# Attention layer of a four-layer image kernel: packed query and key projections, Ln and Exp for the root, a new order of the steps

## The chip, the core and the metric

The kernel runs on one core of a Trainium2 chip. A core has a matrix engine (PE, with the loading of its weights shown apart as PEld), a vector engine (DVE), a scalar engine (ACT), GpSimd (POOL) and a sync engine (SP) that here only starts transfers. Each engine takes its instructions in order. They share an on-chip memory of 128 partitions (SBUF); PE writes its results to a second memory, PSUM, which has eight banks of 512 floats per partition. The metric is the device time of one execution in microseconds.

## The reference

Four layers work on eight images of 56 x 56 positions with 192 channels. Each is a residual step over a group norm: `x = x + layer(group_norm(x))`. The change lies in layer 1, a shifted-window attention with 64 windows of 7 x 7 = 49 positions per image and 6 heads of 32 channels:

```python
x = (x - mu) * jax.lax.rsqrt(var + EPS) * gamma + beta     # over the channels of a position
sx = jnp.roll(x, shift=(-3, -3), axis=(1, 2))              # then cut into windows of 49
qkv = (win @ w_qkv + b_qkv).reshape(-1, N, 3, HEADS, hd).transpose(2, 0, 3, 1, 4)
attn = jnp.einsum('bhnd,bhmd->bhnm', q * scale, k) + bias + mask
attn = jax.nn.softmax(attn, axis=-1)
out = jnp.einsum('bhnm,bhmd->bhnd', attn, v)               # heads side by side again
out = out @ w_proj + b_proj                                # windows put back, rolled back
```

Layer 0 is a gated Toeplitz convolution, layer 2 a depthwise convolution with running averages, layer 3 a convolution with a two-step perceptron.

## The kernel before

The layers run one after the other, with their intermediate images in device memory. Layer 0 has two stages. In the first (`layer0_qv`) products of two projections are made and stored to the arrays `left` and `right`; in the second (`layer0_mix`) blocks of them are loaded (`lt`, `rt`, L454), rearranged by POOL, ACT and DVE (L462), multiplied on PE (L470), and gated and projected (L480 to L579). At the start of `layer0_mix` two blocks are loaded, two operands of each kind are prepared, the large tiles `os` are laid out, and then the weights `w_p` and `w_o` are fetched by POOL's queue (L110). A tile laid out where a tile of the stage before lay must wait for the last user of that place.

**Layer 1** holds an image as 128 rows: two halves of the picture (called streams, s = 0 and 1) of 64 channel rows each, with three channel blocks j in the free dimension. An image is worked off in four groups g; a group has 8 windows in each stream. `layer1_norm` prepares an image ahead of time: `windows` copies and scales it into window order (POOL, and others for the first image), `squares` squares it (ACT), two sets of matmuls with ones (L838, L842, "stat") give sums, `finish` turns the variance into 1/root (L813 on DVE, L815 Sqrt on ACT, L817 reciprocal on DVE), and `scaled` spreads the factors by a matmul (L822) and multiplies (L827, DVE). It is a generator: each `next` does one small piece.

Attention of a group is cut into steps, named by letters:

- Q: one projection of queries or keys for 3 of the 6 heads, 96 output rows, both streams (L880); four of them per group. Query results get their bias and are both copied by ACT (L886); key results go by ACT and DVE (L888, L890).
- V: one of two projections of values (L898), copied by ACT and DVE (L905, L907).
- E: scores of one stream, 48 small products (L916) into the PSUM tile S; then on DVE the added bias and mask (L922) and the maximum (L924), and on POOL the subtraction (L925). E0 is the first, E1 the second.
- X: exponents of one stream (L929, ACT). Y: their sum and its reciprocal (L934, L935, DVE) and the multiplication by it (L936, POOL).
- T: one third of a stream's turn, four transposes (L957) and a copy by ACT or DVE (L962, L964). The first turn of stream 0 is called T0 below.
- P: the mix of values by shares (L971), into two PSUM tiles, one for each half z of the windows, copied by ACT and DVE (L982, L984).
- R: the output projection of one channel block j (L990), then added into the image on DVE (L998) in two pieces, since the roll wraps around. R0, R1, R2 are the three.
- G: statistics of a block of the finished group before (L1001, DVE). There are three of them for a group; a G that finds none left does nothing.
- N: one piece of the next image's norm.

Within a group, Q, V and E already belong to the next group, while X, Y, T, P and R belong to the present one. The order on every engine of this stage is the order in which the program writes the instructions, and that is a string:

```python
plan = "X Q Y V X G Q Y N T T T N Q N P N G V N N T T T N G N N P N Q N R N E N R G E N R".split()
```

PSUM is shared out: S has three banks; three buffers called "mm" go round for Q (2), V (2), stat, scaled and R; two called "et" go round for T and P. A matmul that needs a buffer waits until its last contents have been copied out.

`layer1_weights` prepares weights and biases during layer 0. `gn_finish` makes the scale and shift of a group norm.

Of the kernel before, what the change touches and what calls it, by code (L numbers as in the profile page):

```python
# [19 lines left out]
HC = 96  # L20
TT = 392
# [50 lines left out]
    ("g1", 3), ("be1", 3), ("bq", 2), ("bv", 2), ("bpr", 3),  # L72
# [18 lines left out]
def kernel(ctx: ExitStack, tc: tile.TileContext, a: dict, out: bass.AP):  # L91
# [71 lines left out]
    def gn_finish(mv, sc, sh, pool, psum, ptag):  # L163
# [23 lines left out]
        nc.scalar.activation(sc, over_groups(d, "gh_v"), AF.Sqrt, bias=eps5)  # L187
        nc.vector.reciprocal(sc, sc)
# [395 lines left out]
    def layer0_mix(pool, raws, psum, ops, loaded):  # L584
# [63 lines left out]
        n, gate, first, side, xn = 0, iter(()), iter(()), iter(()), None  # L648
        os = [pool.tile([64 + W, 128, H], F32, name=f"o{k}", bufs=1) for k in range(2)]
        w_p, w_o = (resident(n, nc.gpsimd, pool) for n in ("w_p", "w_o"))  # L650
# [48 lines left out]
    def layer1_weights(pool, psum):  # L699
# [9 lines left out]
        bv = pool.tile([HC, 2], F32, name="bv", bufs=1)  # L709
        for which, t in ((0, bq), (2, bv)):  # L710
            ps = psum.tile([128, 2, 512], F32, name="bias", tag="qv")[:, 0]
            for m in range(2):
                c0 = which * C + HC * m
                for j in range(3):
                    nc.tensor.matmul(
                        ps[0:HC, m:m + 1], w_qkv[0:64, j, c0:c0 + HC], vec("be1", j, 64), start=(j == 0), stop=(j == 2)
                    )
            o = VOFF["bq" if which == 0 else "bv"]
            nc.vector.tensor_tensor(t, ps[0:HC, 0:2], vecs[0:HC, o:o + 2], ALU.add)
        nc.vector.tensor_scalar(bq, bq, HD ** -0.5, None, ALU.mult)  # L720
        yield
        ps = psum.tile([128, 2, 512], F32, name="bias", tag="qv")[:, 0]
        for s in range(2):
            for j in range(3):
                for m in range(2):
                    nc.tensor.matmul(
                        ps[64 * s:64 * s + 64, j:j + 1], w_proj[:, m, 64 * j:64 * j + 64], bv[:, m:m + 1],
# [6 lines left out]
        nc.vector.tensor_scalar(w_qkv[:, :, 0:C], w_qkv[:, :, 0:C], HD ** -0.5, None, ALU.mult)  # L734
# [35 lines left out]
    def layer1_norm(b, x, pool, psum, consts, first=False):  # L770
# [41 lines left out]
        def finish(rows):  # L812
            nc.vector.tensor_scalar(rs[rows], rs[rows], 0.0, 1e-5, ALU.max, ALU.add)  # L813
            yield
            nc.scalar.activation(rs[rows], rs[rows], AF.Sqrt)  # L815
            yield
            nc.vector.reciprocal(rs[rows], rs[rows])  # L817
# [11 lines left out]
        for g0, n in ((0, 1), (1, 1), (2, 2)) if first else ((0, 2), (2, 2)):  # L829
            sqs = []  # L830
            for g in range(g0, g0 + n):
                yield from windows(g)
                sqs.append(pool.tile([128, 2, 3, 4 * WN], F32, name="sq", bufs=2))
# [33 lines left out]
    def layer1_scores(g, xr, pool, psum, S, es, consts):  # L867
# [3 lines left out]
        qk = [pool.tile([HC, 2, 2, TT], F32, name=f"qk{s}", bufs=1) for s in range(2)]  # L871
# [3 lines left out]
        def project(which, m):  # L875
            ps = [psum.tile([128, 512], F32, name="qk_ps", tag="mm", bufs=3)[0:HC, 0:TT] for s in range(2)]
# [891 lines left out]
```

## Time and profile before

| | us |
|---|---|
| median of 3 runs | 5577.13 |
| lowest and highest run | 5567.75, 5584.76 |
| profiled execution, its own time | 5579.16 |
| its span, first to last instruction | 5577.4 |

Busy time per engine in four stretches of the span (the second half of layer 1's last group reaches some 10 us into the fourth):

| stretch, us | what | PE | DVE | ACT | POOL | granted clock |
|---|---|---|---|---|---|---|
| 0 to 755 | layer 0, products | 703.3 | 414.4 | 322.4 | 435.9 | 0.98 |
| 755 to 1951 | layer 0, mix | 1087.1 | 563.0 | 601.2 | 631.0 | 0.97 |
| 1951 to 3010 | layer 1 | 957.1 | 628.0 | 392.0 | 396.0 | 0.95 |
| 3010 to 5577 | layers 2 and 3 | 2321.2 | 1428.7 | 974.1 | 415.8 | 0.95 |

In the profile's lines a group is given as line, engine, operation, output <- input, shape, count. In the timeline each row has its start, its busy time, the engine, the line and, in brackets, how long the engine had been idle and what ended the idle time. "xN" counts instructions on the engine: one matmul of the program is two of them. L numbers are lines of the kernel before.

Some durations of layer 1 in this profile: a query copy on ACT 0.58, a key copy 0.48 on ACT and 0.56 on DVE, the root 0.53, the reciprocal of the variance rows 2.55, a table load on ACT 1.28.

### The profile page before, as it was taken

The page shows a single profiled execution, that of the slowest core. Times are in us where ns is not written, and L with a number is a line of the kernel's source. Part 1 is how long each engine was busy: PE and PEld are TensorE (multiplying, and loading weights), DVE is VectorE, ACT ScalarE, POOL GpSimd, SP SyncE. Part 2 cuts the span into 40 slices and gives each one's busy share as a digit, 9 for nine tenths or more (in the row PEclk, how much of TensorE's full clock was granted, in tenths as well). Part 3 has the DMA queues.
Part 4 walks back from the last instruction along what each step waited for, and adds up shares of the span by engine and source line. Part 5 has one row for each costly group of instructions (what it writes and reads, how often), then busy time and mean ns, then how long its engine had stood idle before and what let it go on. Part 6 is the DMA issues. An engine that isn't in the chain of part 4 may idle for free. (4 is left out here: it accounts for less than half of the span.)

```text
span 5577.4 us, 112511 instructions
## 1 busy us (share of the span) xinstructions
PE 5068.6 (91%) x49038; PEld 3354.8 (60%) x49038; DVE 3034.1 (54%) x4087; ACT 2289.7 (41%) x3052; POOL 1878.7 (34%) x1583
## 2 busy tenths in 40 slices
PE   7999969999999889999997989999788787999999
PEld 6788856666666545555554757776344586444444
DVE  4555534555555455655665868888777313333331
ACT  3444445555555333333332015545476402333333
POOL 5555555555555333433432014333111101101000
PEclk9999989999999989999998989999899898999999
DMA  5998996777777512322314856776687596212211
GB/s 150 240 232 225 222 301 247 274 272 274 274 272 274 166 44 72 82 74 72 84 54 101 286 216 218 241 231 200 163 232 217 218 345 263 68 59 82 78 40 27
DMA packets 533281, 1002.69 MB, mean 180 GB/s; under 512 B 256104, under 2 KB 467780, under 8 KB 501412
## 3 DMA queue, kind: packets, MB, share of 16 engines
q1 hardware_dynamic: 519984, 945.57, 52.9%
q0 software_dynamic: 8560, 40.64, 2.2%
q10 hardware_dynamic: 4244, 9.27, 0.6%
q8 instruction: 386, 6.32, 0.5%
q14 instruction: 107, 0.88, 0.0%
HBM read 665.12 MB, written 346.75 MB: 181 GB/s over the span
## 5 line engine op out<-in xcount | busy, mean ns | idle before, releaser
L462 POOL COPY lc<-lt 128x896 f32<-128x896 f32 (+1 forms) x320 | 617.0, 1937 | 491.5 <-PE op L470 485.8
L429 PE MATMUL qv<-w_qv_sb,x 64*112 64x256 f32 (+1 forms) x5376 | 685.5, 408 | 16.1 <-DVE act L435 12.3
L429 PEld LDWEIGHTS qv<-w_qv_sb,x 64*112 64x112 f32 x5376 | 594.7, 175 | 96.0 <-DVE act L435 22.6
L435 DVE TENSOR_TENSOR act<-qv,b_qv 112x640 f32<-112x640 f32 x448 | 318.6, 753 | 319.7 <-PE qv L429 230.3
L439 ACT ACTIVATE act<-act 112x640 f32<-112x640 f32 x448 | 300.4, 683 | 404.9 <-DVE act L435 394.5
L405 POOL TENSOR_TENSOR qv<-act 112x320 f32<-112x320 f32 x448 | 348.8, 805 | 277.3 <-ACT act L439 195.8
L1360 PE MATMUL ph<-y,w_sb 64*128 64x392 f32 x2304 | 397.7, 498 | 6.5 <-ACT hid L1364 6.5
L470 PE MATMUL op<-rc,lc 128*56 128x56 f32 x9216 | 351.9, 220 | 56.3 <-POOL lc L462 37.9
L470 PEld LDWEIGHTS op<-rc,lc 128*56 128x56 f32 x9216 | 327.1, 134 | 125.3 <-POOL lc L462 56.4
L1371 PE MATMUL po<-hid,w_sb 128*64 128x392 f32 x2304 | 386.3, 494 | 0.0
L1378 DVE TENSOR_TENSOR x<-x,z 128x392 f32<-128x392 f32 x96 | 71.6, 746 | 519.7 <-ACT z L1376 519.7
L880 PE MATMUL qk_ps<-xr,wg 64*96 64x392 f32 x1536 | 334.0, 537 | 1.7 <-DVE xr L827 1.7
L1091 PE MATMUL cv<-zc,wt 128*128 128x224 f32 x1536 | 312.9, 355 | 24.1 <-DMA zc<-pd 24.1
L1091 PEld LDWEIGHTS cv<-zc,wt 128*128 128x128 f32 x1536 | 290.4, 189 | 67.5 <-issue 51.4
L925 POOL TENSOR_TENSOR e<-e,mx 128x1176 f32<-128x1176 f32 x64 | 140.0, 2188 | 565.9 <-DVE mx L924 523.1
L1360 PEld LDWEIGHTS ph<-y,w_sb 64*128 64x128 f32 x2304 | 220.0, 188 | 176.0 <-issue 25.6
L503 PE MATMUL y<-pp,w_o_sb 128*64 128x392 f32 x1536 | 309.1, 499 | 6.4 <-DVE pp L497 6.4
L1106 POOL TENSOR_TENSOR rows<-rows,loc 128x896 f32<-128x896 f32 x96 | 220.5, 2297 | 274.0 <-ACT rows L1102 209.2
L480 PE MATMUL pj<-xn,w_p_sb 64*128 64x392 f32 x1536 | 289.3, 509 | 20.8 <-ACT pp L487 18.6
L1371 PEld LDWEIGHTS po<-hid,w_sb 128*64 128x64 f32 x2304 | 162.6, 137 | 213.8 <-issue 213.8
L462 ACT COPY rc<-rt 128x896 f32<-128x896 f32 (+1 forms) x160 | 280.9, 1755 | 19.5 <-DMA rt<-right 19.5
L497 DVE TENSOR_TENSOR pp<-pp,ot 128x784 f32<-128x784 f32 x128 | 124.1, 969 | 293.6 <-PE ot L492 235.0
(242 smaller groups left out, 9034.0 us busy)
## 6 DMA issues: line engine op xcount, KB each, us to landing
lt<-left SPq DMA_DIRECT2D x72, 1792.0 KB
rt<-right SPq DMA_DIRECT2D x72, 1792.0 KB
left<-qv SPq DMA_DIRECT2D x224, 252.0 KB
right<-qv SPq DMA_DIRECT2D x96, 504.0 KB
wt<-in_band_dram SPq DMA_DIRECT2D x23, 2048.0 KB
zc<-pd SPq DMA_DIRECT2D x187, 232.0 KB
pd<-pt SPq DMA_DIRECT2D x7, 5568.0 KB
bm<-bmask SPq DMA_DIRECT2D x64, 588.0 KB
```

Source lines behind the costliest of these rows:

```text
L405: nc.gpsimd.tensor_tensor(qv[:, s, s0:s1, k], *(acts[s][:, which, 0:n].rearrange("p (s d) -> p s d", d=64) for which in range(2)), ALU.mult,)
L429: nc.tensor.matmul(ps[s][:, which, 0:n], x[64 * s:64 * s + 64, j, bass.ts(i, 2 * W)], w_qv[64 * s:64 * s + 64, j, which, 64 * s0:64 * s1], ...
L435: nc.vector.tensor_tensor(acts[s][:, :, 0:n], ps[s][:, :, 0:n], b_qv[:, :, 64 * s0:64 * s1], ALU.add)
L439: nc.scalar.activation(acts[s][:, :, 0:n], acts[s][:, :, 0:n], AF.Silu)
L462: copy(c[:, 0:nu], raw.rearrange("p (w u d) -> p u d w", u=nu, d=64 // nu)[:, :, d0:d0 + 8])
L470: nc.tensor.matmul(op[64 * u:64 * u + W, i, :], lc[:, u, i], rc[:, u, i], start=True, stop=True)
L480: nc.tensor.matmul(ps[:, s, 0:TT], w_p[64 * s:64 * s + 64, j, 128 * c:128 * c + 128], xn[64 * s:64 * s + 64, j, bass.ts(t, TT)], start=(j ...
L503: nc.tensor.matmul(y[64 * s:64 * s + 64], w_o[:, 2 * g + u, 64 * j:64 * j + 64], pp[:, u, s], start=(u == 0), stop=(u == 1),)
L880: nc.tensor.matmul(in_pairs(ps[s]), wg[64 * s:64 * s + 64, j, c0:c0 + HC], in_slots(xr[64 * s:64 * s + 64], (3 * g + j) * GW), start=(j == ...
L1091: nc.tensor.matmul(dst, wt[:, c4 + i, 128 * q:128 * q + 128], zc[:, :, c4 + i, q:q + NPAIR], start=(q == 0), stop=(q == 1),)
L1360: nc.tensor.matmul(ps[:, s, 0:TT], w0[64 * s:64 * s + 64, j, m * 128:(m + 1) * 128], y[64 * s:64 * s + 64, j, ts], start=(j == 0), stop=(j ...
L1371: nc.tensor.matmul(ps[64 * s:64 * s + 64], w1[:, m, 64 * j:64 * j + 64], hid[:, m, s], start=(m == 0), stop=(m == 5),)
```

## The change

Queries and keys are projected in three steps of 128 output rows instead of four of 96. The columns of the weight matrix are reordered by the host so that step 0 gives queries of heads 0 to 2 and the key of head 5, step 1 keys of heads 0 to 2 and the query of head 5, step 2 queries of heads 3 and 4 and keys of heads 3 and 4. ACT copies stream 0's result, DVE stream 1's, both adding the bias. Since a query and its key must stand on the same rows, a further ACT copy within SBUF moves one part of each step into the tiles `q2` and `k2`.

```diff
-        def project(which, m):
+        def project(m):
...
-            for s in range(2):
-                if which == 0:
-                    nc.scalar.activation(qk[s][:, 0, m], ps[s], AF.Identity, bias=bq[:, m:m + 1])
-                elif s == 0:
-                    nc.scalar.copy(qk[s][:, 1, m], ps[s])
-                else:
-                    nc.vector.tensor_copy(qk[s][:, 1, m], ps[s])
+            nc.scalar.activation(qk[:, m, 0], ps[0], AF.Identity, bias=bq[:, m:m + 1])
+            nc.vector.tensor_scalar(qk[:, m, 1], ps[1], bq[:, m:m + 1], None, ALU.add)
+            i, src, dst = ((1, slice(96, 128), slice(64, 96)), (0, slice(96, 128), slice(64, 96)), (1, slice(64, 128), slice(0, 64)))[m]
+            nc.scalar.copy(moved[i][dst], qk[src, m])
...
-            for y, hh, r, p, z in np.ndindex(2, 2, 3, 2, 2):
+            for hh, y, r, p, z in np.ndindex(2, 2, 3, 2, 2):
                 at = WN * (2 * (2 * y + p) + z)
+                rows = slice(HD * r, HD * r + HD)
+                q = moved[0][rows, s] if hh and r == 2 else qk[rows, 2 * hh, s]
+                k = moved[1][rows, s] if hh else qk[rows, 1, s]
```

The mix P puts heads 0 to 3 of one half z on 128 rows and heads 4 and 5 beside them on 64 rows; it goes through the heads by the turn that they come from. Its copies become two per engine. The output projection R takes 128 rows at once and the remaining 64 rows of both halves on different rows of the array, into two PSUM tiles, and its add into the image becomes three pieces.

```diff
-            po = [psum.tile([128, 512], F32, name="po", tag="et", bufs=2)[0:HC, 0:TT] for _ in range(2)]
-            for y, p, hh, r, z in np.ndindex(2, 2, 2, 3, 2):
-                k = 2 * y + p
+            po = [psum.tile([128, 512], F32, name="po", tag="et", bufs=2) for _ in range(2)]
+            for r, y, p, hh, z in np.ndindex(3, 2, 2, 2, 2):
+                k, h = 2 * y + p, 3 * hh + r
+                row, col = (HD * h, 0) if h < 4 else (64 * z + HD * (h - 4), 4 * WN)
...
+                copy(oa[s][:, z], po[z][:, 0:4 * WN])
+                copy(oa[s][rows, 2], po[z][rows, 4 * WN:8 * WN])
...
-            ps = psum.tile([128, 512], F32, name="pr", tag="mm", bufs=3)[:, 0:TT]
-            for m in range(2):
+            out = []
+            for z, (tag, bufs) in enumerate((("mm", 3), ("et", 2))):
+                out.append(psum.tile([128, 512], F32, name=f"pr{z}", tag=tag, bufs=bufs)[:, 0:4 * WN])
                 for s in range(2):
                     nc.tensor.matmul(
...
+                        w_proj[:, 0, 64 * j:64 * j + 64], by_row(oa[s][:, z]), start=True, stop=False,
                     )
...
+            for z in range(2):
+                rows = slice(64 * z, 64 * z + 64)
+                for s in range(2):
+                    nc.tensor.matmul(
+                        out[z][64 * s:64 * s + 64].rearrange("p (i w j) -> p i w j", i=7, j=7),
+                        w_proj[rows, 1, 64 * j:64 * j + 64], by_row(oa[s][rows, 2]), start=False, stop=True,
+                    )
+            for z, w0, w1, c0 in ((0, 0, 28, 3), (1, 0, 25, 31), (1, 25, 28, 0)):
```

The third turn of a stream takes an "mm" buffer instead of an "et" buffer. One over root becomes exp(-0.5 ln v), on ACT alone, in `finish` and, within layer 1, in `gn_finish`; the table that holds both functions is loaded once, at the end of layer 0.

```diff
-            tp = psum.tile([128, 512], F32, name="et_ps", tag="et", bufs=2)
+            tag, bufs = ("mm", 3) if i == 2 else ("et", 2)
+            tp = psum.tile([128, 512], F32, name="et_ps", tag=tag, bufs=bufs)
...
-            nc.scalar.activation(rs[rows], rs[rows], AF.Sqrt)
-            yield
-            nc.vector.reciprocal(rs[rows], rs[rows])
+            nc.scalar.activation(rs[rows], rs[rows], AF.Ln)
+            yield
+            nc.scalar.activation(rs[rows], rs[rows], AF.Exp, scale=-0.5)
...
         layer0_mix(pool, blocks, psum, ops, loaded)
+        nc.scalar.preload_act_table_set("natural_log_exp_and_others")
```

The order string is new, with one Q less and 13 N; in the start of layer 1 one Q goes too. With two groups at once, `layer1_norm` now copies both groups' windows before it squares either. In `layer0_mix` the weights are fetched before the tiles `os` are laid out. `layer1_weights` follows the new order of the columns.

```diff
-        for kind in "QVQVQQEE":
+        for kind in "QVQVQEE":
...
-        plan = "X Q Y V X G Q Y N T T T N Q N P N G V N N T T T N G N N P N Q N R N E N R G E N R".split()
+        plan = "X Q N Y V N X G Q N Y N T T T P N V N N T T T P G Q N R N E N R N G E N R N".split()
...
+        w_p, w_o = (resident(n, nc.gpsimd, pool) for n in ("w_p", "w_o"))
         os = [pool.tile([64 + W, 128, H], F32, name=f"o{k}", bufs=1) for k in range(2)]
-        w_p, w_o = (resident(n, nc.gpsimd, pool) for n in ("w_p", "w_o"))
```

## The prediction

> **What bounds the kernel now.** I read four views, in this order. The page first: the matrix engine is busy 91% of the span, so the question is which of its work shrinks and which waits take its place.
>
> ```profile
> PE 5068.6 (91%) x49038; PEld 3354.8 (60%) x49038; DVE 3034.1 (54%) x4087; ACT 2289.7 (41%) x3052; POOL 1878.7 (34%) x1583
> ```
>
> The chain that ended last carries only 30% of the span and lies in the later layers, so it doesn't price layer 1. Layer 1 runs from 1951 to about 3020 us. I cut one image of it at the end of each E0 (the scores of stream 0), which gives four segments:
>
> ```profile
> 2231.20:2259.25 28.05, 26.59 (x532) 16.27 (x528) 16.94 (x25) 9.77 (x16) 8.76 (x4) 1.00 0.23 67
> 2259.25:2288.57 29.32, 26.91 (x533) 16.45 (x529) 16.93 (x25) 12.07 (x20) 16.92 (x22) 1.00 0.45 111
> 2288.57:2325.90 37.33, 34.20 (x580) 18.91 (x577) 18.65 (x28) 13.85 (x25) 16.21 (x20) 0.91 0.32 78
> 2325.90:2360.58 34.68, 31.56 (x541) 17.81 (x537) 25.39 (x35) 12.27 (x19) 8.75 (x4) 0.95 0.19 54
> ```
>
> The columns are length, then busy time of PE, PEld, DVE, ACT, POOL, then granted clock, DMA share, GB/s. An image is 129.4 us. PE bounds it, but not alone: the plain segment has 1.5 us of PE gaps, and the third and fourth ran partly at half clock (0.91 and 0.95). The timeline of the second segment's first half shows where those gaps come from:
>
> ```profile
> 2262.14 0.74 DVE L998 SCALAR_TENSOR_TENSOR x<-pr,bpr,x 128x371 f32<-128x371 f32 x2
> ...
> 2266.23 1.37 DVE L934 TENSOR_REDUCE sm<-e 128x24 f32<-128x1176 f32 x1
> ...
> 2266.46 2.27 PE L898 MATMUL v_ps<-wg,xr 64*128 64x192 f32 x23 [0.51 <-DVE x L998]
> ...
> 2268.65 2.19 POOL L936 TENSOR_TENSOR e<-e,sm 128x1176 f32<-128x1176 f32 x1
> ...
> 2268.82 2.61 PE L880 MATMUL qk_ps<-xr,wg 64*96 64x392 f32 x11
> ...
> 2271.36 1.09 PE L957 MATMUL et_ps<-ident,e 128*128 128x128 f32 x8
> ```
>
> V waits because its PSUM buffer is the one that R2 used, and DVE empties R2 only after both maxima. T0, the turn of stream 0, needs the chain scores, add, maximum, subtract, exponent, sum, reciprocal, multiply (POOL ends at 2270.84). It starts at 2271.36, 12.1 us after E0's end, because Q1 ended there: PE just outlasts the chain, by about 0.5 us.
>
> **The change on PE.** A project of Q is 2.15 us from start to start (2.22 busy). Four become three: -2.15 per group. R takes 1.59 from start to start. In the new R, 8 instructions of 196 columns run in pairs and 8 in fours, on four quarters of the array. Layer 0 shows that fours run together: 16 instructions of 392 columns in 1.50 us, four steps of about 0.33.
>
> ```profile
> 2256.37 1.66 PE L990 MATMUL pr<-oa,w_proj_sb 96*64 96x392 f32 x8
> ...
> 1900.28 1.50 PE L569 MATMUL yl<-pp,w_o_sb 64*64 64x392 f32 x16
> ```
>
> L898 shows 192-column pairs at 2.15/12 = 0.18 us a step. The new R is six such steps plus 0.15 to start: 1.25 us, -0.34, three times. So PE loses 3.2 us per group. E, P and T keep their counts of instructions and, in their new order, use as many distinct parts of the array; I cost their order at nothing.
>
> **On the other engines.** A column costs about 1 ns on DVE, a further instruction about 0.17 to 0.2 us (the 371- and 21-column adds of L998: 599 and 229 ns, 0.74 as a pair). Each R gets a third add: +0.17. The copies of P become two of about 0.35 each on DVE (+0.15), on ACT two of 0.31 (+0.13). Each Q now puts one 0.56 copy on DVE and one 0.53 on ACT, where the query projects had both on ACT. Each also has a new ACT copy of 784 columns inside SBUF. The trace has no such copy. Nearest rows: square of 588 at 0.70, exponent of 1176 at 1.21, so 0.87; the scattered ACT copy of 896 columns (L462, 1.83) is the upper end. I take 0.87, as this one is contiguous. Behind that copy stand, on ACT, the next V's copy and the turn's copies, and it waits for DVE's half of Q: DVE's lateness is handed to ACT, then PE. Per image, the 2.55 us reciprocal and two table loads of 1.28 go, for one Exp of about 0.53; the gain is in the fourth segment's wait. The third statistics call of a group (0.56) now falls between R1's adds and E1's add; before, the slot in that place found the list empty.
>
> **Walking one plain segment** with start-to-start times, E0's end at 0. DVE: E0 add 0.1, max 1.58, R1 adds 2.88, statistics 3.7, E1 add 4.2, max 5.7, R2 adds 7.0, Q0 copy 7.8, sum 8.3, reciprocal 9.7. POOL multiplies 10.1 to 12.3, so T0 can start at 12.4; before, it was ready at 11.6. PE: R1, E1, R2, Q0 are done at 6.3; V waits 1.1 us for R2's buffer (now 7.4), Q1 waits 0.6 for V's copy, and ends at 12.3. PE's saving is thus spent in this half: 12.4 against 12.1. In the second half T (third turn no longer waiting for a bank) ends at 14.05, but P waits 1.35 us: both banks must be emptied, DVE's turn copy stands behind Q1's copy and the second sum (12.9 to 14.6), and ends at 15.3. P 15.4, V 16.4, T 18.55, P 20.5 (0.3 waited), Q2 21.5, R0 23.65, E0 24.9 to 26.2. The moved copy for E0's second half of heads is ready at 25.2, in time. The same walk over the old order gives 12.1 and 28.0, as measured. New: **26.2 against 28.05**.
>
> Second segment: 26.2 and 0.4 that PE waited for nothing visible: 26.6 (29.32). Third: the statistics matmuls (2.1) lie before Q0, whose second buffer waits for R2; T0 at 14.95, the segment 28.75; I keep 1.4 of waiting for nothing visible (DMA share is 1.06 there) and 1.7 of half clock: 31.85 (37.33). Fourth: the same statistics; DVE, Ln and Exp in series let the first scaling start at 17.1, PE idle 2.2 before it; the four scalings' DVE multiplies (1.57 each) delay both turn copies: 34.5, and 1.2 of half clock: 35.7 (34.68, a loss). Sum 120.35 against 129.38: 9.0 per image.
>
> **Half clock: trace against rule.** The granted clock fell to 0.50 after windows of 3.41 us in which PE was still partly busy:
>
> ```profile
> 2291.48:2294.89 3.41, 2.02 (x97) 1.23 (x95) 1.39 (x4) 0.97 (x1) 2.19 (x1) 1.00 1.06 262
> 2294.89:2301.72 6.83, 6.83 (x51) 2.85 (x34) 5.40 (x7) 0.23 (x1) 3.18 (x4) 0.50 0.56 146
> 2315.37:2318.78 3.41, 2.32 (x106) 1.71 (x104) 1.20 (x3) 1.57 (x3) 2.10 (x5) 1.00 0.02 5
> ```
>
> 2.02 busy (59%) was followed by half clock, 2.32 (68%) was not. The Trainium skill ("TensorE: Matmul & The Clock Gate", Part 1) says that the clock is halved after an idle window of some 3.4 us. By that rule no wait above (2.2 at most) costs clock: 117.5 per image, 20 us more gain over seven images. The measurement decides: a wait above about 1.37 us inside one window is enough, and the new waits of 1.35 sit at that edge. I keep two events per image.
>
> **Outside the steady images.** The eighth image has no norm: three segments of 1.85 and three Rs, 6.6. The start of layer 1 has three finish steps in the open: one loses a table load, root and reciprocal (1.28 + 0.53 + 2.59) for two of 0.53, two lose 3.12 for 1.06, and one project goes: 3.3 + 2.1 + 2.1 + 2.15 = 9.6. The weights of the mix, fetched before the big tiles are laid out, no longer stand behind the stores:
>
> ```profile
> 782.18 0.37 SPq L589 DMA_DIRECT2D x<-in_x_dram  x1
> 782.72 0.59 POOL L110 DMA_DIRECT2D w_p_sb<-in_w_p_dram  x1 [22.07 <-DMA right<-qv]
> ...
> 785.61 3.40 PE L470 MATMUL op<-rc,lc 128*56 128x56 f32 x64 [23.17 <-POOL lc L462]
> ...
> 787.23 0.52 SPq L454 DMA_DIRECT2D lt<-left  x1
> ```
>
> POOL's 22 us go, but what is late next is SP: the load of x still waits for all stores (782.18), and the third block's lt and rt stand behind it. They can go 4.6 to 5.1 earlier, and the weights' 1.37 MB leave a stretch that moves 420 GB/s. 4 us, between 0 (the DMA engines are 0.8 to 0.9 busy before 782, so the weights may delay the stores as much) and 5.
>
> **Sum.** 7 x 9.0 + 6.6 + 9.6 + 4 = 83. From the profiled execution's 5579.2 (span 5577.4, 2 above the median of the runs, 5577.1): **5496 us**.
>
> **Rivals.** (a) PE alone bounds (its 91% speaks for it; the walked waits on DVE against it): then 3.2 per group go and the half clock with its waits too, some 16.5 per image: 7 x 16.5 + 8 + 9.6 + 5 = 138, 5441. Chance 0.20. (b) DVE's row takes everything back: segments stay as they were, only start and mix gain, 10 to 20: about 5563. For it: DVE's row already costs 0.3 us in the first half; against: the second half is 2.2 shorter in the walk. Chance 0.13. (c) Slower, by half clock: if the waits before V and before P are 0.3 us longer than walked (a moved copy of 1.2 us is enough), both cross the 59% edge in every group: eight events per image for two, six more of 1.7 us over eight images is 82, and 0.3 x 2 x 32 = 19 of waiting: 101 - 83 = +18, 5597. It decides from five to six more events per image on. For it: 1.35 lies at the edge. Against: 1.1 and 1.35 seldom fall whole into one window. Chance 0.12. (d) Forecast, gains of 40 to 120: 0.55; its own range is 5459 to 5539. That the tables don't stay loaded isn't a rival: the instruction order has no table load left inside layer 1.
>
> A measurement of this kernel tells 0.3% (17 us) from no change. Faster: 0.55 + 0.20 + half of (b) = 0.82; same 0.06; slower 0.12. The range leaves out the tail of (a) and most of (c): 5430 to 5575.
>
> **What would show it.** Right: Q at 36 instructions a group; R near 1.25 from start to start; E0-to-T0 about 12.4 and T0-to-E0 13.8 in plain segments; PE's waits before V and P named DVE; POOL's 22 us gone and the third block's lt issued near 782.6. Wrong: R at 1.6 or more, moved copies above 1.2 us, more than three stretches of half clock per image, or plain segments below 25.5 (then the DVE row was walked too slow) or above 27.5.

## The result, and the profile after

The changed kernel takes **5494.1 us**, the median of four runs (5487.4 to 5505.7), against 5580.7 for the kernel before beside it: ratio 0.9851, 95% interval 0.9827 to 0.9875. The prediction was 5496, with a range of 5430 to 5575.

The profiled execution took 5505.7 us (span 5503.9), 12 us above that median. By its trace the difference of the two spans, 73.5 us, is made up so (times from the first to the last instruction named):

| stretch | before | after | difference | predicted |
|---|---|---|---|---|
| up to the first product of layer 1's statistics | 1951.5 | 1962.7 | +11.2 | -4 (mix weights) |
| from there to the end of the first E0 | 44.0 | 32.7 | -11.3 | -9.6 |
| from there to the end of the last scores | 999.4 | 928.4 | -71.0 | -69.6 |
| the rest | 2582.5 | 2580.2 | -2.3 | 0 |

So layer 1 gained 82.3 us where the sum had 79.2. The last section comes back to the 11 us ahead of it.

The page's line of the engines, of the kernel after; the matrix engine's share stays at 91% because span and work shrank together:

```profile
PE 4998.8 (91%) x49428; PEld 3379.9 (61%) x49428; DVE 3053.1 (55%) x4273; ACT 2311.1 (42%) x3109; POOL 1877.9 (34%) x1583
```

The windows view of the kernel after, cut at the ends of E0 as before. The columns are again length, busy time of PE, PEld, DVE, ACT and POOL, granted clock, DMA share and GB/s; the rows are plain, second, third, fourth:

```profile
2215.46:2241.89 26.43, 24.32 (x544) 16.95 (x540) 18.00 (x31) 10.99 (x18) 8.76 (x4) 1.00 0.25 71
2241.89:2268.33 26.44, 24.16 (x545) 16.89 (x541) 18.00 (x31) 12.04 (x20) 16.89 (x22) 1.00 0.24 71
2268.33:2297.14 28.81, 26.86 (x567) 17.52 (x565) 19.29 (x33) 14.01 (x25) 16.25 (x20) 1.00 0.57 149
2297.14:2332.51 35.37, 31.45 (x577) 20.13 (x573) 25.03 (x41) 14.10 (x25) 8.76 (x4) 0.95 0.19 53
```

The plain segment went from 28.05 to 26.43 us. PE's busy time in it fell by 2.3 us, its gaps grew from 1.5 to 2.1: the saving on PE didn't come through whole. The third segment gained most (37.33 to 28.81) and runs at full clock. The fourth became longer: 35.37 for 34.68 here, and 36.7 for 34.2 in the mean of the seven images that have a norm beside them. The first of these images takes 127.7 us, since its second segment stays at 34.4 (33.8 before): norm steps left over from the start of layer 1 still run in it. The other six take 116.7 to 121.8. The mean of the seven is 119.7 (129.3 before), where 120.35 was predicted.

The timeline of a plain segment of the kernel after shows where the gaps lie. E0 ends at 2332.51; columns are start, busy time, engine, line and operation, and in brackets the idle time before it and what ended it:

```profile
2339.89 2.22 PE L901 MATMUL v_ps<-wg,xr 64*128 64x192 f32 x24 [0.91 <-DVE x L1004]
...
2342.58 2.19 POOL L935 TENSOR_TENSOR e<-e,sm 128x1176 f32<-128x1176 f32 x1 [0.75 <-DVE sm L934]
...
2344.84 1.53 PE L956 MATMUL et_ps<-ident,e 128*128 128x128 f32 x12
...
2347.17 0.27 PE L971 MATMUL po<-et,v 49*32 49x49 f32 x2 [0.80 <-ACT et L961]
...
2347.80 1.20 PE L971 MATMUL po<-et,v 49*32 49x49 f32 x94 [0.36 <-DVE et L963]
2348.93 2.22 PE L901 MATMUL v_ps<-wg,xr 64*128 64x192 f32 x24
...
2356.26 0.94 PE L990 MATMUL pr<-oa,w_proj_sb 128*64 128x196 f32 x8
2357.12 0.59 PE L997 MATMUL pr<-oa,w_proj_sb 64*64 64x196 f32 x8
```

Counted from E0's end: V starts at 7.4 after 0.91 of waiting for R2's adds on DVE, POOL's multiply runs from 10.1 to 12.3, T0 starts at 12.3, P comes through at 15.3 when DVE's copy of the second turn is done, V1 at 16.4, R0 at 23.75. These marks agree with the walk, each within 0.2 us. The third turn now runs on with the other two (x12 in one row), where it stood apart before.

The fourth segment, first in the windows view of the kernel after, around its wait for the first scaling:

```profile
2311.37:2314.78 3.41, 1.22 (x4) 0.47 (x4) 2.28 (x4) 1.55 (x3) 1.06 (x2) 1.00 0.02 5
2314.78:2318.20 3.42, 3.42 (x69) 3.09 (x70) 2.16 (x3) 1.17 (x2) 1.41 (x1) 0.51 0.00 0
```

And the two rows of its timeline that make the wait:

```profile
2313.18 0.53 ACT L822 ACTIVATE rs<-rs 128x392 f32<-128x392 f32 x1
2313.76 0.92 PE L827 MATMUL rstd<-rs,sel 32*128 32x392 f32 x2 [2.19 <-ACT rs L822]
```

The Exp ends at 16.6 us after E0's end and the scaling's product starts then (17.1 was predicted, with a wait of 2.2; it is 2.19). PE was busy for 1.22 of the 3.41 us of the first window above, and the next window ran at half clock (0.51).

### The profile page after: what moved, and what is told of

It is laid out like the page before. It is cut to its first block, busy times and chain, and to the rows that moved or that the text cites. A ratio compares the mean times of both kernels' runs of the same rounds, so it can differ in the third digit from the quotient of the medians.

```text
span 5503.9 us, 113538 instructions
## 1 busy us (share of the span) xinstructions
PE 4998.8 (91%) x49428; PEld 3379.9 (61%) x49428; DVE 3053.1 (55%) x4273; ACT 2311.1 (42%) x3109; POOL 1877.9 (34%) x1583
## 5 line engine op out<-in xcount | busy, mean ns | idle before, releaser
L432 PEld LDWEIGHTS qv<-w_qv_sb,x 64*112 64x112 f32 x5376 | 592.5, 176 | 112.5 <-DVE act L438 32.2
L473 PE MATMUL op<-rc,lc 128*56 128x56 f32 x9216 | 354.5, 221 | 55.1 <-ACT rc L465 38.2
L1115 DVE TENSOR_TENSOR_SCAN sums<-dec,rows 64x896 f32<-64x896 f32 x96 | 278.5, 2901 | 1.3
```

The source lines that it names most:

```text
L432: nc.tensor.matmul(ps[s][:, which, 0:n], x[64 * s:64 * s + 64, j, bass.ts(i, 2 * W)], w_qv[64 * s:64 * s + 64, j, which, 64 * s0:64 * s1], ...
L473: nc.tensor.matmul(op[64 * u:64 * u + W, i, :], lc[:, u, i], rc[:, u, i], start=True, stop=True)
L1115: nc.vector.tensor_tensor_scan(_reversed(sums[0:64]), d[0:64], _reversed(rows[0:64]), 0.0, ALU.mult, ALU.add)
```

## The experiments

All times are medians beside runs of the kernel before on the same chip. "Layer 1" is the length from the first product of the statistics to the end of the last scores, in the profiled execution. An engine's "row" is the order of work that it goes through within a segment.

| kernel | us | ratio to before, 95% | layer 1 |
|---|---|---|---|
| before | 5577 to 5581 | 1 | 1043.4 |
| after | 5494.1 | 0.9851 (0.9827 to 0.9875) | 961.1 |
| weights of the mix undone | 5506.7 | 0.9864 (0.9851 to 0.9878) | 960.7 |
| roots undone | 5529.0 | 0.9907 (0.9893 to 0.9920) | 994.1 |
| third turn's bank undone | 5564.6 | 0.9971 (0.9960 to 0.9983) | 1014.2 |
| P and R undone | 5524.8 | 0.9900 (0.9884 to 0.9917) | 971.8 |
| fillings undone | 5484.4 | 0.9836 (0.9819 to 0.9852) | 949.5 |
| only Q and K packed | 5566.1 | 0.9977 (0.9970 to 0.9984) | 1022.6 |
| only the third turn's bank | 5560.2 | 0.9967 (0.9958 to 0.9976) | 1017.0 |
| statistics late | 5494.4 | 0.9853 (0.9839 to 0.9868) | 954.3 |
| moved copy late | 5483.6 | 0.9826 (0.9798 to 0.9853) | 949.3 |
| moved copy late, bank undone | 5506.3 | 0.9870 (0.9838 to 0.9902) | 962.0 |
| scalings spread | 5474.5 | 0.9813 (0.9799 to 0.9828) | 938.6 |
| scalings spread, row shortened | 5433.9 | 0.9737 (0.9721 to 0.9754) | 896.9 |

### One part undone at a time

**The weights of the mix.**

```diff
-        w_p, w_o = (resident(n, nc.gpsimd, pool) for n in ("w_p", "w_o"))
         os = [pool.tile([64 + W, 128, H], F32, name=f"o{k}", bufs=1) for k in range(2)]
+        w_p, w_o = (resident(n, nc.gpsimd, pool) for n in ("w_p", "w_o"))
```

> The changed kernel, with the weights of layer 0's mix fetched behind the o tiles again, as before. The prediction's term: the stores and loads start 4 us later, 5498 us against the 5494 of the changed kernel. First theory, from the trace of after (the third block's first product came 9.5 us later than before, although POOL's wait was gone): what POOL gains the DMA engines take back, so POOL's wait of some 22 us at the weights returns and the time stays within 5 us of 5494. Second theory: the early fetch itself costs those 9.5 us, and without it the time is about 5484.

5506.7 us: the intervals of both kernels overlap, so the median doesn't decide. The trace does: POOL's wait ahead of the weights is back (20.77 us), and yet the mix, from its first to its last copy of rc, takes 1131.9 us, against 1132.3 after and 1132.6 before. In the ten kernels here that fetch the weights early it takes 1129.6 to 1132.7, in the four that fetch them late 1131.9 to 1132.6. The part is worth nothing that these traces can tell. In the kernel after, POOL issues the weights early and then waits for the third block all the same:

```profile
770.14 0.59 POOL L109 DMA_DIRECT2D w_p_sb<-in_w_p_dram  x1
...
808.68 3.32 POOL L465 COPY lc<-lt 128x896 f32<-128x896 f32 x2 [22.35 <-DMA lt<-left]
```

The load of x, which has to wait for the stores on SP, goes out at 795.38, 30.3 us after the mix began (26.6 before). In the ten kernels it goes out 28.9 to 31.6 us after, in the four 25.3 to 27.9: with the weights ahead of them the stores end later. The second theory, that the early fetch costs 10 us, falls too.

**The roots.**

```diff
-            nc.scalar.activation(rs[rows], rs[rows], AF.Ln)
+            nc.scalar.activation(rs[rows], rs[rows], AF.Sqrt)
             yield
-            nc.scalar.activation(rs[rows], rs[rows], AF.Exp, scale=-0.5)
+            nc.vector.reciprocal(rs[rows], rs[rows])
...
-        nc.scalar.preload_act_table_set("natural_log_exp_and_others")
```

> The changed kernel, with the roots and reciprocals of layer 1 as before (Sqrt on ACT, reciprocal on DVE, tables loaded as needed). Theory of the prediction: at the start of layer 1 the three finish steps lose 3.3 + 2.1 + 2.1 = 7.5 us, and in each of seven images the first scaling waits for a table load (1.28), a root (0.53) and a reciprocal (2.55) instead of 0.53 twice, 3.3 later, all of it in the fourth segment: 7.5 + 23 = 31, about 5525 us. Rival: in the images other work covers the row, and only the start counts: 5502 us. Second rival: PE's longer wait also brings half clock that is not there now, another 1.7 us per image: 5537 us.

`gn_finish` goes back to root and reciprocal too. 5529.0, 35 more (expected 31). The trace splits it as expected: E0's end in the start of layer 1 comes 39.9 us after the first statistics product instead of 32.7 (7.2; 7.5 expected), and the rest of layer 1 is 25.9 longer (23 expected), nearly all of it in the fourth segments, 38.2 to 41.3 us for 35.3 to 40.1. The half clock in these segments doubles, from 44 to 82 us in all, so the second rival has a part in it too. Of the view of one fourth segment of this kernel, the pieces of the wait:

```profile
2331.59 1.28 ACT L820 ACT_TABLE_LOAD   x1
...
2334.44 2.59 DVE L822 RECIPROCAL rs<-rs 128x392 f32<-128x392 f32 x1
...
2337.18 1.17 PE L827 MATMUL rstd<-rs,sel 32*128 32x392 f32 x2 [3.32 <-DVE rs L822]
```

**The third turn's bank.**

```diff
-            tag, bufs = ("mm", 3) if i == 2 else ("et", 2)
+            tag, bufs = "et", 2
```

> The changed kernel, with the third turn back in the bank of the first. It then waits for ACT's copy of the first turn, some 0.4 us. Theory: in the first half of a segment P waits for DVE's copy in any case, so only the second half loses 0.4 us per group, 13 us in all: 5507 us. Rival, PE alone bounds: both halves lose it, 26 us: 5520 us. Second rival: P waits for copies anyway in both halves, no change: 5494 us.

5564.6: 70 us, more than either theory gave, and four fifths of what the whole change had brought. Plain segments take 27.9 to 28.1, and where half clock falls into them 29.5. The timeline of a plain segment of this kernel, the second half of its front:

```profile
2612.90 0.84 ACT L893 COPY q<-qk 32x784 f32<-32x784 f32 x1 [0.77 <-DVE qk L891]
2613.77 0.59 ACT L961 COPY et<-et_ps 128x512 f32<-128x512 f32 x1
...
2614.41 0.65 PE L956 MATMUL et_ps<-ident,e 128*128 128x128 f32 x4 [1.24 <-ACT et L961]
...
2615.10 0.59 ACT L961 COPY et<-et_ps 128x512 f32<-128x512 f32 x1 [0.74 <-PE et_ps L956]
2615.74 1.83 PE L971 MATMUL po<-et,v 49*32 49x49 f32 x94 [0.43 <-ACT et L961]
```

The third turn waits 1.24 us, not 0.4, since ACT's copy of the first stands behind Q1's moved copy, and P then waits for ACT's copy of the third instead of DVE's of the second. Both halves lose: about 0.8 us each. 1.5 per group is 48 us; half clock, which now lies in four plain segments too and for 10.2 us in four of the fourth ones, makes up the rest of the 53 us of the trace. The run medians differ by more, 70, in part because the profiled execution lies 6.8 us under the median here and 11.6 over it in the kernel after.

**P and R.** The functions mix and project(j) of layer 1's mix, and the layout of the projection's weights and of bv, as they were before:

```diff
-        oa = [pool.tile([128, 3, 4 * WN], F32, name=f"oa{s}", bufs=1) for s in range(2)]
+        oa = [pool.tile([96, 2, TT], F32, name=f"oa{s}", bufs=1) for s in range(2)]
...
-            for z, w0, w1, c0 in ((0, 0, 28, 3), (1, 0, 25, 31), (1, 25, 28, 0)):
+            for w0, w1, c0 in ((0, 53, 3), (53, 56, 0)):
```

> The changed kernel, with P and R as before (two halves of 96 rows, two adds of 371 and 21 columns per R, one copy per P and engine, the old order of P's products); Q, the bank of the third turn, the fillings and the roots stay changed. R is then 1.59 us from start to start and not 1.39, DVE has 0.17 less per R and 0.15 less per P. If PE alone bounds: 3 x 0.2 per group, 19 us more, 5513 us. If DVE's row sets T0, as in the prediction: the two Rs ahead of T0 give back 0.34 us per group, the third costs 0.2 and P, which needs all three turns at once again, about 0.3 in the second half: 0.16 per group, 5 us more, 5499 us. If the old layout is better for the row than reckoned, below 5490 us.

5524.8 by the runs (31 more than after; its own runs scatter over 22 us), 10.7 more in layer 1 by the trace: plain segments are 26.94, 0.51 longer. T0 comes at 12.6 instead of 12.3, so DVE's fewer adds gave nothing back there: PE brings R1 and E1 later, and DVE gets its work later. The rest is in the second half. The 0.51 per plain segment lies nearer to the theory of PE (0.6) than to that of DVE's row (0.16): work of PE ahead of the row counts as well as work on it.

**The fillings.**

```diff
-        plan = "X Q N Y V N X G Q N Y N T T T P N V N N T T T P G Q N R N E N R N G E N R N".split()
+        plan = "X Q Y V X G Q Y N T T T N P N G V N N T T T N G N N P N Q N R N E N R G E N R".split()
```

> The changed kernel, with the old order of the fillings (the N steps of the next image's norm and the statistics G), with one Q less. In plain segments the norm has no steps and the order of all else is the same, so they stay at 26.43 us in each theory. Theory: the new places of N are what keeps the third segment free of half clock and of the wait for instructions (28.5 against the 31.85 of the prediction, which took these over from the old order): some 3 us per image, 20 us in all, 5515 us. Rival: the shorter project and the free bank did that, not the places, and the time stays at 5494 us.

5484.4, 10 us less, against the expectation; the intervals overlap, but layer 1 is 11.6 us shorter too. Three things come together. The theory held for the third segments: they are longer in six images of seven, by 2 to 7 us (31.1 to 35.3 now; 25 us in all), and a stop of PE for nothing that the profile shows (the "wait for instructions" of the expectation) is back in five of them. The run with the statistics late, below, shows that the place of a G is enough to bring such stops. The fourth segments are better by 3.5 us or more in six (31.8 to 32.1), where the scalings stand behind the first turns. And the expectation was wrong that plain segments stay: the old string has a fourth G, so the three calls of the statistics are used up before the stretch between R1 and E1, and the plain segment is 25.97. The new fillings are no gain as a whole.

### The parts alone, from the kernel before

The bank alone is the edit of above the other way round, in the kernel before.

> The kernel before with the packed queries and keys alone: the weights of the mix, the roots, the bank of the third turn, P and R and the order of the fillings as before (one Q less in the plan, the one between the turns and P). If the parts add up, what undoing them one by one cost (about 0, 33, 70 and 29) is lost together: 5494 + 132 = 5626 us, slower than before. Theory of one path: the saved project had covered the wait of P for the turns' copies, so with the third turn in the old bank the second half of a segment gains nothing (walked: T0 at 12.2, E0's end at 28.2 against 28.05), and only the start of layer 1 gains some 10 us: about 5575 us.

> The kernel before, with the third turn's bank alone changed. Theory of one path: the fourth project of before lies between T and P and covers the copies in the first half, so there only the turn's own wait goes (0.24); in the second half the turn's 0.24 and P's 0.47 go: 0.9 us per group at most, 30 us: 5550 us. Rival, the parts are worth the same wherever they stand: 70 us, 5510 us. Second rival, the chain of DVE and POOL sets T0 and takes it back: 5575 us.

5566.1 and 5560.2: 13 and 19 us gained, where 5575 and 5550 were expected. (Only Q keeps the new order of copies and squares in the norm.) The parts don't add: from the top the bank is worth 70 us, from below 19. Only Q has plain segments of 27.7, or 29.3 to 29.5 where half clock falls into them (28.2 walked, 28.05 before): the project that went had covered P's wait for the turns. The bank alone has 27.08, 0.97 less than before (0.9 at most was expected), and in both, half clock stays in most of the third and fourth segments.

### The row of DVE and ACT

> The changed kernel, with the third call of the statistics (0.56 us on DVE) moved from between R1's adds and E1's add to behind the second P, where DVE stands idle. Theory, DVE's row sets T0: V's wait of 0.9 for R2's buffer and T0 come 0.56 us earlier in every group, and P, which waits for DVE's copy, too: 31 x 0.56 = 17 us less, 5477 us, plain segments 25.9. Rival, PE bounds the segment: nothing, 5494 us and 26.43.

```diff
-        plan = "X Q N Y V N X G Q N Y N T T T P N V N N T T T P G Q N R N E N R N G E N R N".split()
+        plan = "X Q N Y V N X G Q N Y N T T T P N V N N T T T P G G Q N R N E N R N E N R N".split()
```

5494.4: no gain in the time, though the plain segments did what DVE's row says, 25.97 for 26.43, V's wait 0.44 for 0.91. Layer 1 is 6.7 us shorter by the trace instead of 17: part of what was gained is lost in the third segments, three of which take 31.4 to 33.2 where they took 28.5 to 28.8. First the waits view of this kernel around one of them (engine, line, what was waited for: us in total, times, longest):

```profile
PE S L916 <- issue: 2.1, 1, 2.1
```

And its windows view there, in windows of the granted clock:

```profile
2381.10:2384.51 3.41, 2.00 (x95) 1.31 (x91) 3.04 (x5) 0.82 (x2) 0.90 (x1) 1.00 1.07 226
2384.51:2391.34 6.83, 6.02 (x49) 2.48 (x53) 3.54 (x5) 0.00 (x0) 3.62 (x3) 0.50 1.05 276
```

In the middle of E1 PE stood still for 2.1 us for nothing that the profile shows, at a DMA share of 1.07; the window was 59% busy, and the next two had half clock. A row cut by 0.46 us doesn't pay if PE then meets such a stretch.

Why does it meet one? The moved call also lets transfers go: SP's loads of a later image wait for the last G of the image before, and go out 0.06 us behind it. In the kernel after that is 4.2 us behind E0's end (2385.44), when E1 is done:

```profile
2389.05 0.56 DVE L1007 BATCH_NORM_STATS2 gh_st<-x 128x6 f32<-128x392 f32 x1
2389.67 2.28 SPq L761 DMA_DIRECT2D x<-x  x2
```

With the statistics late it is 2.9 us ahead of it (2380.48), and E1 runs among them:

```profile
2376.50 1.04 DVE L1007 BATCH_NORM_STATS2 gh_st<-x 128x6 f32<-128x392 f32 x2
2377.60 3.21 SPq L761 DMA_DIRECT2D x<-x  x5
```

What PE then lacks can be read from the trace's records of single transfers. The page of this kernel counts the transfers of the queue that brings PE's instructions:

```profile
q8 instruction: 389, 6.37, 0.5%
```

Each is a block of 16,384 bytes. PE has 99,560 instructions in this trace, 256 for each block; in the kernel with only Q packed it is 383 blocks for 98,068. Seven of the fourteen kernels here let the loads go ahead of E1: before, fillings undone, only Q, only the bank, statistics late, and the two spread ones. Between the first statistics product and the last scores they have 28 stops of 0.9 us or more for nothing that the profile shows, all in third segments. Every one stands, within one instruction, at the same place of a block of 256, and ends 1.3 to 1.8 us after a block has landed. That block's transfer had started 1.9 to 5.7 us after PE passed the same place of the block before, with the DMA engines 0.86 to 1.11 busy meanwhile; where they are idle it starts after 0.9 us (median of 493). The other seven kernels have no such stop. So PE waits for its next instructions, whose transfer starts late when loads fill the DMA engines, and the small products of E1 and R use up a block in a few us.

**The moved copy.** Does it lie on the path? A rival of the prediction had supposed so.

```diff
-            nc.scalar.copy(moved[i][dst], qk[src, m])
+            late = lambda: nc.scalar.copy(moved[i][dst], qk[src, m])
+            if m == 1:
+                waiting.append(late)
+            else:
+                late()
...
-        plan = "X Q N Y V N X G Q N Y N T T T P N V N N T T T P G Q N R N E N R N G E N R N".split()
+        plan = "X Q N Y V N X G Q N Y N T T T M P N V N N T T T P G Q N R N E N R N G E N R N".split()
```

> The changed kernel, with Q1's moved copy (0.84 us on ACT) behind the three turns' copies of the first half instead of ahead of them. Theory: it is not on the path, since P also waits for DVE's copy of the second turn, which stands behind the second sum and comes last (15.3 us after E0's end): no change, 5494 us, plain segments 26.43. Rival: ACT's lateness is what holds P, and 0.8 us per group go: 26 us, 5468 us.

> As m_late, and the third turn back in the bank of the first, as in u_turn. In u_turn the third turn waited 1.24 us for ACT's copy of the first, which stood behind the moved copy, and P for ACT's copy of the third. Theory: there the moved copy is on the path; behind the turns it lets P go when DVE's copy ends, 0.7 us per group earlier: 31 x 0.7 = 22 us less than u_turn, 5543 us, plain segments 27.3. Rival: the bank alone costs the 70 us, 5564 us and 28.0.

5483.6 and 5506.3. With the new bank the plain segments stay at 26.43, as expected. In the timeline of that kernel ACT's copies are now early, and P waits for DVE all the longer:

```profile
2570.87 0.59 ACT L970 COPY et<-et_ps 128x512 f32<-128x512 f32 x1 [0.64 <-PE et_ps L965]
...
2572.45 0.63 DVE L972 COPY et<-et_ps 128x512 f32<-128x512 f32 x1
...
2573.14 1.20 PE L980 MATMUL po<-et,v 49*32 49x49 f32 x94 [1.23 <-DVE et L972]
```

The 11 us by which it is faster all the same aren't in the row: the additional M in the list that fills the start of layer 1 lets four more norm steps run there (6.1 us of the start), and the rest is in the fourth segments. With the old bank the plain segments are 27.2 (27.3 expected), the second ones stay at 28.0, and yet the time falls by 58 us (52 in layer 1), where 22 were expected from the walk: the half clock of the plain segments and most of that of the fourth goes as well, and the start has the same gain of 6.8. So the bank's 70 us were the bank and the moved copy together; with the copy out of the way the bank is worth 22 (5506.3 against 5483.6; their intervals overlap, and layer 1 differs by 12.7 in the traces, since the fourth segments are shorter with the old bank).

### A version that beats both

> The changed kernel with the three calls of the statistics as in g_late, and the four scalings of the next image's norm no longer in one segment: the first stands behind the first P of the fourth segment, the other three follow in the plain one, two of them behind P and one behind R0. Theory: the fourth segment's loss is PE's wait for the first scaling, the half clock after it and DVE's multiplies (1.57 each) ahead of the turns' copies; it falls from some 35 to 26 + 2.1 (statistics) + 0.5 = 29 us, the plain one gains three scalings on PE (1.5): 4.4 us less per image, 31 us in all, 5463 us. Rival: the multiplies delay DVE's row wherever they stand, 4.7 us in the plain segment, and nothing is gained: 5490 us.

```diff
+            "X Q N Y V N X G Q N Y N T T T P N V N N T T T P G G Q N R N E N R N E N R N",
+            "X Q N Y V N X G Q N Y N T T T P N V N N T T T P G G Q N R N E N R N E N R N",
+            "X Q N Y V N X G Q N Y T T T P N V T T T P G G Q R E R E R",
+            "X Q Y V X G Q Y T T T P N V T T T P N G G Q R N E R E R",
...
-                if g == 3:
-                    run(steps)
```

> As spread, and the row ahead of T0 and P shortened: both copies of Q0 on ACT, the second stream's exponent ahead of V's copy and its sum ahead of Q1's copy, the first V's copies swapped between ACT and DVE, and Q1's moved copy behind the turns' copies. Theory, DVE's row and not PE sets T0 and P: walked, V waits 0.4, T0 starts at 11.2 instead of 12.3, P at 13.0 instead of 15.3, E0's end at 24.0 (26.43): third 26, fourth 27, plain 26, second 24.3, 103 us per image against 118.9: 118 us less, 5376 us. Rival, the row was not the bound once G is late (25.97): plain segments stay above 25.5, 5440 us. Second rival: the wait for instructions at full DMA share and the half clock after it grow with a faster PE, as in the third segment of g_late: 5400 us.

```diff
-            nc.vector.tensor_scalar(qk[:, m, 1], ps[1], bq[:, m:m + 1], None, ALU.add)
+            if m == 0:
+                nc.scalar.activation(qk[:, m, 1], ps[1], AF.Identity, bias=bq[:, m:m + 1])
+            else:
+                nc.vector.tensor_scalar(qk[:, m, 1], ps[1], bq[:, m:m + 1], None, ALU.add)
...
-            for s, copy in enumerate((nc.scalar.copy, nc.vector.tensor_copy)):
+            for s, copy in enumerate((nc.scalar.copy, nc.vector.tensor_copy)[::1 if k0 else -1]):
...
+            "X Q Y X V G Y Q T T T M P N V N N N T T T N N P N G G Q N R N E N R N E N R N",
+            "X Q Y X V G Y Q T T T M P N V N N N T T T N N P N G G Q N R N E N R N E N R N",
+            "X Q Y N X V N N G Y Q T T T M P N V T T T P G G Q R E R E R",
+            "X Q Y X V G Y Q T T T M P N V T T T P N G G Q R N E R E R",
```

The spread gave 5474.5 (5463 expected): the fourth segment fell to 29 (as expected), the plain one rose to 28.5 or more (27.5 expected) and holds half clock in three images. With the row shortened it is **5433.9**, 144 us under the kernel before and 60 under the changed one. Its windows view, in the order plain, second, third, fourth:

```profile
2197.79:2225.47 27.68, 27.04 (x550) 17.78 (x546) 21.76 (x36) 11.46 (x19) 8.76 (x4) 1.00 0.23 68
2225.47:2250.62 25.15, 24.15 (x544) 16.87 (x540) 18.10 (x31) 12.40 (x21) 16.91 (x22) 1.00 0.30 89
2250.62:2278.75 28.13, 26.49 (x569) 17.50 (x565) 18.90 (x32) 14.48 (x26) 16.27 (x20) 1.00 0.56 140
2278.75:2306.92 28.17, 27.31 (x570) 18.13 (x566) 20.18 (x34) 14.47 (x26) 8.77 (x4) 1.00 0.22 67
```

Full clock in all four. An image is 108.4 to 109.7 us in four of seven and 112.5 to 115.3 in the others. The 5376 of the walk was too low by 58: in the timeline of a segment of this kernel T0 starts at 11.95 and not 11.2, because Q1 ends only then (Q1 waits for V's copy, V 0.44 for R2); P comes at 13.4 (13.0). PE is the bound there again. In three of the images the third segment still takes 31.6 to 32.1, with half clock; in two of these it follows a stop like those above.

## Why the prediction came out right

**The mechanism.** The claim was that PE's saving of 3.2 us per group comes through only in part: DVE's row sets T0 and P, and the second half gains. What the runs show: the marks of the walk hold (T0 12.33 for 12.4, V1 16.4 for 16.4, R0 23.75 for 23.65, E0's end 26.43 for 26.2), and one call of 0.56 us taken off DVE's row moved the plain segment by 0.46, with PE's work unchanged. That is also what rules out the rival in which PE alone bounds; the gap to it is real, as the last kernel shows by taking part of it. The row is not DVE's alone, though: with P and R undone PE has 0.6 us more work per group and DVE less, and the plain segment is 0.51 longer. PE's R1 and E1 stand at the head of the row.

**The number.** That 5496 and 5494.1 lie 2 us apart is in part luck: errors of both signs cancel, and the profiled execution, from which the terms below are read, took 5505.7.

**Terms that were mis-sized**, with what they measured:
- R, from start to start: 1.25 predicted, 1.39 measured (0.87 for the eight instructions in pairs and 0.52 for the eight in fours, where 0.72, 0.36 and 0.15 to start were put). Three times 0.14 per group, of which the second half shows 0.1 to 0.2.
- PE's saving per group: 3.2 predicted. From start to start Q gives 2.15 and three R of 0.20 give 0.6, so 2.75. And P's order, put at nothing, costs a little: its run of 94 products takes 1.20 in the timeline above, and 1.08 with P and R undone and in the kernel before:

```profile
2253.21 1.08 PE L971 MATMUL po<-et,v 49*32 49x49 f32 x94 [0.47 <-ACT et L962]
```

- The third segment: 31.85 predicted, 28.5 to 28.8 in six images of seven. The reserve of 1.4 for waits for nothing visible and 1.7 for half clock, taken over from before, wasn't used: worth some 3 us per image. In five of those images the loads now start behind E1, and the stop that they brought doesn't come (the sixth has no load there). The prediction counted what the moved G costs DVE and missed that it holds these loads back.
- The fourth: 35.7 predicted, 35.3 to 40.1, mean 36.7. The wait for the scaling was 2.19 as walked; half clock came once to twice, in one image for 17 us.
- The second: 26.6 predicted for all, 26.4 measured in six images, 34.4 in the first. With the two above that makes 119.7 per image for 120.35.
- The mix's weights: 4 predicted (0 to 5), 0 measured. The lower end was right: POOL issues earlier, but the load behind the stores on SP goes out 3.7 us later after the start of the mix.
- The start: 9.6 predicted, 11.3 measured; the roots' share 7.5 against 7.2.
- The moved copy: 0.87 against 0.84. Copies of Q with the bias 0.62 on DVE and 0.59 on ACT for 0.56 and 0.53.

**What it missed.** The third turn's bank appears in it only as a clause ("no longer waiting for a bank"), and E, P and T "at nothing". The bank is the part on which the others depend: without it the rest brings 15 us of 86. The prediction had the right end state, so its sum is right, but the parts have no worth of their own that could be added: 19 us from below, 22 or 70 from above. It also took the calls of the statistics and the fillings as given; undone, the fillings as a whole cost nothing, and moving the last statistics call saves 0.46 us in each plain segment.

**The rivals.** DVE taking everything back (5563) didn't come. The packed Q alone gives about that time (5566), but there PE waits for ACT's copies of the turns in the bank that they share, so the likeness of the numbers is chance. Half clock in every group (5597) didn't come: of the stretches of half clock in the seven images none lies in a plain segment; the waits of 0.91 and 1.16 brought none. By the rule that the prediction quoted (the Trainium skill, "TensorE: Matmul & The Clock Gate", Part 1: the clock is halved after an idle window of some 3.4 us) neither the window at 2311.37, 36% busy, nor the one at 2381.10, 59% busy, would have cost clock. The trace has half clock behind both. But the edge at 59%, which the prediction took from two windows, doesn't hold either. In the kernel before itself, a window that was 64% busy was followed by half clock, and one that was 60% busy was not:

```profile
2598.68:2602.09 3.41, 2.19 (x10) 1.13 (x12) 2.94 (x3) 0.59 (x1) 1.69 (x1) 1.00 0.00 0
2602.09:2605.50 3.41, 3.41 (x11) 1.36 (x8) 1.39 (x3) 0.47 (x1) 0.00 (x0) 0.50 0.00 0
...
2851.27:2854.68 3.41, 2.03 (x14) 1.28 (x12) 3.38 (x4) 2.08 (x4) 2.18 (x1) 1.00 0.01 2
2854.68:2858.09 3.41, 3.37 (x15) 1.49 (x16) 2.29 (x4) 0.27 (x1) 0.00 (x0) 1.00 0.00 0
```

In other kernels a window that was 52% busy kept full clock (P and R undone, at 2550.68), and one that was 76% busy lost it (moved copy late, bank undone, at 2544.02). What else decides in between stays open.

## What to carry to other kernels

When an instruction that covered a wait is removed, find the wait and remove it too, or the saving turns into idle time: here packing Q paid 13 us until the third turn had its own bank. Undo parts one at a time from the new kernel and add them one at a time to the old; where the two don't agree, two parts share a path, and the timeline of that kernel names the copy that they share. Steps of a second stream (here the norm's scalings) go where the engine that takes them has a gap, spread over segments, and not all into the first free places of one: that took 16 us off layer 1 here (938.6 for 954.3). Before a call is moved, ask what waits for it: here a call of 0.56 us on DVE decided when a load starts, and so what PE did beside that load.

## What was not expected of the hardware

- PE stopped for 0.9 to 5.2 us in the middle of runs of products, with no wait that the profile's rows show, when the DMA share was near 1. The 28 stops of seven kernels all stand where PE goes on to a block of instructions that has just landed. That the block's transfer starts late because of the loads is read from the times; no run changes the loads alone.
- Half clock followed windows of 3.41 us in which PE was 36%, 59%, 64% and even 76% busy, while others of 52% and 60% kept full clock. In the seven images of the kernel after it lasted 3.4 to 17 us at a time.
- Up to the first statistics product the changed kernel took 11 us longer, though nothing so early in layer 0 was meant to change. Nearly 7 of them come at one place, about 150 us in: PE waits for DVE, DVE for POOL, and POOL 14.01 us for a store of left, where in the kernel before it waited 5.18 for one of right. Other kernels with the packed Q had from 0 to 7 us there. That wait is 5.2 to 6.0 us in three traces (before, only the bank, only Q) and 10.3 to 14.3 in the other eleven, so it may not be mere scatter; but no part undone alone brings it back to 5, and which one moves these stores stays open. It is one reason why medians and traces differ by some 10 us in places, and why layer 1 in the trace was used to price the parts.
